# Cross-attention with LayerNorm: score matmuls cut into 32x64 tiles, two kinds of elementwise work exchanged between ScalarE and VectorE

## The chip, the cores and the metric

The kernel runs on one core of one Trainium2 chip. The metric is device time in microseconds (us) from the start to the end of one launch; the kernel before takes 534.93 us (median of 3 runs, 534.4 to 535.43). PE is TensorE (PEld its weight loads), DVE is VectorE, ACT is ScalarE, POOL is GpSimd, SP is SyncE, which issues most of the DMAs. A measurement of this kernel can tell about 0.2% from no change.

## What is computed

Four sequences of 2048 queries of width 512 attend to 77 keys each, with 16 heads of 32. The result goes through an output matrix, the input is added, and each row is normalised and scaled.

```python
qs = (x @ wq).reshape(B, 2048, 16, 32).transpose(0, 2, 1, 3)
ks_ = (ctx @ wk).reshape(B, 77, 16, 32).transpose(0, 2, 1, 3)
vs = (ctx @ wv).reshape(B, 77, 16, 32).transpose(0, 2, 1, 3)
scores = einsum('bhqd,bhkd->bhqk', qs, ks_) / sqrt(32)
scores = where(mask[:, None], -inf, scores)
attn = einsum('bhqk,bhkd->bhqd', softmax(scores), vs)
out = attn.transpose(0, 2, 1, 3).reshape(B, 2048, 512) @ wo + x
mu, var = mean(out), mean((out - mu) ** 2)
y = (out - mu) / sqrt(var + 1e-5) * gamma + beta
```

## The kernel before

The 8192 rows are 64 tiles of 128 queries. Tile t is cut out of a group of four tiles (512 queries) for the query projection, and out of a block of two tiles for everything behind the softmax. Matmuls that need more than one pass of precision are written as three products of high and low parts.

The stages of one tile, by function:

- `q_visit(g, m)` (L163): 12 matmuls, which project 512 queries of group g on 128 of the 512 columns, into one PSUM bank. `q_evac(g, m)` (L174) copies the bank to SBUF, 128x512 floats, on VectorE.
- `scores(t)` (L274): 16 matmuls, one for each head, into four PSUM banks. A head's 32 rows of the query columns sit on 32 of the 128 partitions; each matmul uses 32 rows and all 128 columns of the array, its weights are the 128 queries and 77 keys stream through. Heads j = 0 to 3 use the four row strips and write to four banks. In the trace each of these float matmuls is two weight loads and two matmuls.
- `maxima(t, lo, hi)` (L291), VectorE: for each head, one instruction adds the mask, writes the negated scores to SBUF and gives the maximum; an accumulator read follows it.
- `exps(t, lo, hi)` (L308), ScalarE: the exponential of each head with its sum.
- `recip(t)` on VectorE, `normalise(t)` (L324) on GpSimd: the probabilities over the sum, one instruction of 128x1232.
- `transp(t)` on VectorE and `regroup(b)` with 12 DMAs on SP's queue: probabilities with keys on partitions.
- `av(b)` (L374): probabilities times values for two tiles, in 96x32 tiles of the array. `av_hi` on ScalarE and `av_lo` on VectorE split the result.
- `o_proj(t)` (L436): 12 matmuls with the output matrix. `residual(t)` adds the input rows, `moments(t)` (L456) takes mean and variance on VectorE; for the second tile of a block, four short GpSimd instructions (L468 to L471) make `rn`: the factor 1/sqrt(var + eps) and the offset -mean times factor, one each for every row.
- `scale(t)` (L473): o = factor * o + offset for the 128x512 rows of a tile, in place in SBUF, on ScalarE. `affine(t)` (L479): times gamma, plus beta, two GpSimd instructions. `store(t)`: DMA to the output.
- `cast_xT` (ScalarE) and `split_xT` (L151, GpSimd, one instruction of 128x1024): high and low part of the transposed input for later projections.

The schedule is written out by hand: every engine works through its instructions in the order in which the program emits them. A loop (L583 to L687) runs for u = 0, 2, ..., 52; one turn works on tiles u and u+1 in the first stages, on u-6 and u-5 in the output projection, and, from u = 8 on, on u-8 and u-7 in `scale`, `affine` and `store`. In one turn VectorE gets: `maxima(u)` with a `q_evac` between its two halves, `residual`, `moments`, `transp(u-1)`, a second `q_evac`, `maxima(u+1)` with `recip(u)` in it, `av_lo`, `residual`, `av_lo`, `transp(u)`, `moments`, `recip(u+1)`. GpSimd gets: `normalise(u-1)` at the turn's start, `split_xT`, `affine(u-8)`, `normalise(u)`, `affine(u-7)`, the four instructions for `rn`. ScalarE gets: `cast_xT`, twelve exponentials of u, `scale(u-8)`, `scale(u-7)`, the last four of u, four of u+1, two `av_hi`, and twelve of u+1. TensorE gets: `scores(u)`, `o_proj(u-6)`, `q_visit`, `scores(u+1)`, `av`, `o_proj(u-5)`, `q_visit`. All PSUM tiles come from eight banks in turn, 14 in one turn of the loop, so that a stage waits for the reader of the tile that was given out eight before.

Three times, VectorE prepares the mask of the next sequence in a turn of its own (`mask_bias`, u = 12, 28, 44, and `mask_nan`, u = 14, 30, 46), between `transp(u-1)` and `maxima(u+1)`.

The last ten tiles and the output stages that are still open follow the string `ORDER` (L45), one word for each step, with other placements; `k` there is `scale`, `q` is `q_evac`.

Of the kernel before, what the change touches and what calls it, by code (L numbers as in the profile page):

```python
# [13 lines left out]
ALU = mybir.AluOpType  # L14
# [3 lines left out]
P = 128  # L18
D = 512
H = 16  # L20
HD = 32
NK = 77
# [4 lines left out]
GH = 4  # L27
# [3 lines left out]
BLK = 256  # L31
# [36 lines left out]
def xattn_layernorm(  # L68
# [15 lines left out]
    nc = tc.nc  # L84
    NB = mask.shape[0]
    TPB = mask.shape[2]
# [8 lines left out]
    def bank(name):  # L95
        return ps.tile([P, 512], F32, tag="mm", name=name)
# [8 lines left out]
    kct = const.tile([P, NG, NB, NK2], F32, name="kct")  # L105
# [28 lines left out]
    def keys_of(h):  # L134
        return slice(TAIL_K, NK2) if h % 2 == 0 else slice(0, NK)

    fx, gx, qd, qp, bat, pts = {}, {}, {}, {}, {}, {}
    scs, nmax, sums, bts, at, pas = {}, {}, {}, {}, {}, {}
    od, pos, mvs, rns, vd, ris, ends = {}, {}, {}, {}, {}, {}, []


    def load_xT(g, c):
        fx[g, c] = sb.tile([P, 2, GRP], F32, tag="xtf", name=f"xtf_{g}_{c}")
        nc.sync.dma_start(fx[g, c], xT[g, :, c : c + 2])

    def cast_xT(g, c):
        if g not in gx:
            gx[g] = [sb.tile([P, NC_D, GRP], F32R, tag=t, name=f"{t}_{g}") for t in ("xth", "xtl")]
        nc.scalar.copy(gx[g][0][:, c : c + 2], fx[g, c])  # L149

    def split_xT(g, c):  # L151
        h, l = (a[:, c : c + 2] for a in gx[g])
        nc.gpsimd.tensor_tensor(l, fx.pop((g, c)), h.bitcast(F32), ALU.subtract)  # L153
# [17 lines left out]
            for i in range(2):  # L171
                q_rows(pq[:, i * BLK : (i + 1) * BLK], m + i, 0, slice(BLK, GRP))

    def q_evac(g, m):  # L174
        pq = qp.pop((g, m))
        if g:
            nc.vector.tensor_copy(qd[g][:, m, :], pq)
        else:
            nc.vector.tensor_copy(qd[0][:, m : m + 2, BLK:], pq.rearrange("p (m r) -> p m r", m=2))


    def keys_part(pks, m, cs):
# [42 lines left out]
    def values_evac(b):  # L225
        pv = vd.pop(b)[:NK2].rearrange("p (q a d) -> p q a d", a=2, d=HD)
        for a in range(2):
            nc.vector.tensor_scalar(
                vsb[:, b].rearrange("p (q a d) -> p q a d", a=2, d=HD)[:, :, a], pv[:, :, a], vm[:, a, 0:1], None, ALU.mult
            )  # L230
# [42 lines left out]

    def scores(t):  # L274
        qs = qd[t // 4]
        rs = slice((t % 4) * P, (t % 4) * P + P)
        nmax[t] = sb.tile([P, H], F32, tag="nm", bufs=3, name=f"nm_{t}")
        sums[t] = sb.tile([P, H], F32, tag="sum", bufs=3, name=f"sum_{t}")
        sc = scs[t] = [bank(f"sc_{t}_{j}") for j in range(GH)]
        for g in range(NG):  # L280
            for j in range(GH):
                q = slice(HD * j, HD * (j + 1))
                nc.tensor.matmul(  # L283
                    sc[j][:, g * NK : (g + 1) * NK],
                    qs[q, g, rs],
                    kct[q, g, t // TPB, keys_of(j)],
                    start=True,
                    stop=True,
                )

    def maxima(t, lo, hi):  # L291
        pb = pbuf[t % NPB]
        mb = bat[t // TPB][0]
        nm = nmax[t]
        for h in HEADS[lo:hi]:
            g, j = divmod(h, GH)
            nc.vector.tensor_tensor_reduce(  # L297
                pb[:, h // 2, (h % 2) * NK : (h % 2 + 1) * NK],
                scs[t][j][:, g * NK : (g + 1) * NK],
                mb[:, t % TPB, keys_of(h)],  # L300
                -1.0,
                3.0e38,
                ALU.add,
                ALU.min,
                accum_out=nm[:, h : h + 1],
            )

    def exps(t, lo, hi):  # L308
        pb = pbuf[t % NPB]
        for h in HEADS[lo:hi]:  # L310
            nc.scalar.activation(  # L311
                pb[:, h // 2, (h % 2) * NK : (h % 2 + 1) * NK],
                pb[:, h // 2, (h % 2) * NK : (h % 2 + 1) * NK],
                AF.Exp,
                bias=nmax[t][:, h : h + 1],
                scale=-1.0,
                accum_out=sums[t][:, h : h + 1],
            )
# [100 lines left out]
    def load_x(t):  # L419
        if t < NT - 8:  # L420
            od[t] = sb.tile([P, D], F32, tag="o", bufs=8, name=f"o_{t}")
        elif t < NT - 4:
            if not ends:
                ends.append(sb.tile([P, NC_D, GRP], F32R, tag="xth", name="o_end").bitcast(F32))
            od[t] = ends[0][:, t % 4]
        else:
            if t % 2 == 0:
                ends.append(sb.tile([P, 2, GRP], F32, tag="xtf", name=f"o_end_{t}"))
            od[t] = ends[-1][:, t % 2]
        nc.sync.dma_start(od[t], x[t * P : (t + 1) * P, :])  # L430
# [42 lines left out]
    def scale(t):  # L473
        o = od[t]
        tt = t % 2
        rn = rns[t // 2]
        nc.scalar.activation(o, o, AF.Identity, bias=rn[:, 1, tt : tt + 1], scale=rn[:, 0, tt : tt + 1])

    def affine(t):  # L479
        o = od[t]  # L480
        nc.gpsimd.tensor_tensor(o, o, gam, ALU.mult)  # L481
        nc.gpsimd.tensor_tensor(o, o, bet, ALU.add)  # L482
# [52 lines left out]
    for c in range(NC_D):  # L535
        split(x0h[:, c], x0l[:, c], f0[c // 2 * 2][:, 0, c % 2])
        split(wqh[:, c], wql[:, c], stage_a[:, 0, c])
        for m in range(NG):
            for n, (w, r) in enumerate(((wqh, x0h), (wqh, x0l), (wql, x0h))):
# [4 lines left out]
                    start=(c == 0 and n == 0),  # L544
                    stop=(c == NC_D - 1 and n == 2),
# [30 lines left out]
    def visits(u):  # L576
        return early.get(u) or [divmod(u + 5, 4)] * (u + 5 < 4 * NGRP)

    def pieces(u):
        return casts.get(u) or [((u + 8) // 4, u % 4)] * (u + 8 < 4 * NGRP)  # L580

    evac = [(0, 0)]
    for u in range(0, 2 * CUT, 2):  # L583
        n = u // 2
        m, k = divmod(u, TPB)

        for q in pieces(u + 2):
            if u >= 4:
                load_xT(*q)
        for t in (u - 4, u - 3):  # L590
            if t >= 0:
                load_x(t)
        scores(u)
        maxima(u, 0, H // 2)
        for q in evac:
            q_evac(*q)
        maxima(u, H // 2, H)
        for q in pieces(u):
            cast_xT(*q)
        exps(u, 0, 3 * H // 4)  # L600
        for v in list(vd):
            values_evac(v)
        for q in pieces(u):
            split_xT(*q)
        if u == 0:
            mask_bias(0, slice(1, TPB))
            split_wv()
        if u >= 6:
            o_proj(u - 6)
        for v in {2: (0,), 4: (2, 3)}.get(u, ()):  # L610
            values(v)
        for q in visits(u):
            q_visit(*q)
        if u >= 6:
            residual(u - 6)
            moments(u - 6)
        if u == 4:
            transp(2)
        if u:
            transp(u - 1)  # L620
            regroup(n - 1)
        if u >= 8:
            scale(u - 8)
            scale(u - 7)
        exps(u, 3 * H // 4, H)
        if u >= 8:
            affine(u - 8)
        for q in visits(u):
            q_evac(*q)
        if u == 0:  # L630
            load_wo()
            nc.gpsimd.memset(ident, 0.0)
            nc.gpsimd.affine_select(ident, ident, [[-1, P]], ALU.not_equal, 1.0, base=0, channel_multiplier=1)
        if u == 2:
            split_wo(0)
            split_wo(1)
        if k == TPB - 6 and m + 1 < NB:
            load_mask(m + 1)
        if k == TPB - 4 and m + 1 < NB:
            mask_bias(m + 1)  # L640
        if k == TPB - 2 and m + 1 < NB:
            mask_nan(m + 1)

        scores(u + 1)
        maxima(u + 1, 0, 3 * H // 4)
        recip(u)
        maxima(u + 1, 3 * H // 4, H)
        exps(u + 1, 0, H // 4)
        normalise(u)
        if u >= 8:  # L650
            affine(u - 7)
        for v in list(vd):
            values_evac(v)
        if u >= 4:
            av(n - 2)
            av_hi(n - 2, 0)
            av_hi(n - 2, 1)
        exps(u + 1, H // 4, H)
        if u >= 5:
            o_proj(u - 5)  # L660
        if u >= 4:
            av_lo(n - 2, 0)
        if u >= 5:
            residual(u - 5)
        if u >= 4:
            av_lo(n - 2, 1)
        if u != 2:
            transp(u)
        for v in {2: (1,)}.get(u, ()):
            values(v)  # L670
        evac = visits(u + 1)
        for q in evac:
            q_visit(*q)
        if u == 2:
            load_xT(*pieces(4)[0])
        if u >= 5:
            moments(u - 5)
        if u == 0:
            mask_nan(0)
        if u == 2:  # L680
            split_wo(2)
            split_wo(3)
        recip(u + 1)
        normalise(u + 1)
        if u >= 8:
            store(u - 8)
            store(u - 7)  # L687
# [87 lines left out]
```

## Time and profile before

| | |
|---|---|
| median of 3 runs | 534.93 us |
| span of the profiled execution | 533.1 us |
| PE busy | 522.3 us (98%) |
| DVE busy | 486.2 us (91%) |
| ACT busy | 459.6 us (86%) |
| POOL busy | 400.7 us (75%) |
| score matmuls (L283) | 2048 records, 72.5 us |
| copies of projected queries (L177) | 60, 669 ns each |
| `scale` (L477) | 48, 807 ns each |

The profiled execution's span is 1.8 us under the median of the timed runs. Busy time is the union of the instructions of an engine, which overlap their neighbours a little; the pitch from one start to the next is what an instruction costs in a row of its kind. Rows of a timeline give start, duration, engine, line, operation and tile, and in brackets the idle time before the instruction with what ended it. The chain of waits follows the work that ended last backwards.

### The profile page before, as it was taken

The page shows a single profiled execution, that of the slowest core. Times are in us where ns is not written, and L with a number is a line of the kernel's source. Part 1 is how long each engine was busy: PE and PEld are TensorE (multiplying, and loading weights), DVE is VectorE, ACT ScalarE, POOL GpSimd, SP SyncE. Part 2 cuts the span into 40 slices and gives each one's busy share as a digit, 9 for nine tenths or more (in the row PEclk, how much of TensorE's full clock was granted, in tenths as well). Part 3 has the DMA queues.
Part 4 walks back from the last instruction along what each step waited for, and adds up shares of the span by engine and source line. Part 5 has one row for each costly group of instructions (what it writes and reads, how often), then busy time and mean ns, then how long its engine had stood idle before and what let it go on. Part 6 is the DMA issues. An engine that isn't in the chain of part 4 may idle for free.

```text
span 533.1 us, 16107 instructions
## 1 busy us (share of the span) xinstructions
PE 522.3 (98%) x4810; PEld 399.1 (75%) x4810; DVE 486.2 (91%) x2592; ACT 459.6 (86%) x2215; POOL 400.7 (75%) x363
## 2 busy tenths in 40 slices
PE   8999999999999999999999999999999999999994
PEld 6977777777777777777777777777777777776672
DVE  5689989999998889889998998889999989999897
ACT  6687799999899999998899999998899999998600
POOL 0626547998798988887899888888799888665751
PEclk9999999999999999999999999999999999999997
DMA  8934667788677887787677787867687775849744
GB/s 300 402 120 111 202 173 195 222 232 226 176 187 213 227 215 208 208 226 201 179 213 214 208 221 217 232 165 211 191 216 216 219 191 159 219 129 281 226 138 157
DMA packets 58695, 109.96 MB, mean 206 GB/s; under 512 B 9392, under 2 KB 11056, under 8 KB 58608
## 3 DMA queue, kind: packets, MB, share of 16 engines
q1 hardware_dynamic: 55424, 102.64, 68.6%
q0 software_dynamic: 2304, 5.24, 3.5%
q10 hardware_dynamic: 880, 1.05, 0.7%
q8 instruction: 38, 0.62, 0.5%
q14 instruction: 49, 0.40, 0.2%
HBM read 41.79 MB, written 16.78 MB: 110 GB/s over the span
## 4 chain that ended last, share of the span: by engine, by line
PE 88%; DMA 5%; DVE 4%; issue 1%; SPq 1%; ACT 0%; DVEq 0%
PE pq L160 32%; PE po L445 30%; PE sc L283 12%; PE pa L381 9%; DMA PT<-B 2%; PE pv L221 2%; DMA out<-o 2%; PE pk L186 1%; DVE B L351 1%; DVE pbuf L297 1%; DMA stage_a<-wq 1%; PE pq L540 1%; DVE o_end L504 1%; DVE o_end L501 1%; SPq L363 0%
## 5 line engine op out<-in xcount | busy, mean ns | idle before, releaser
L311 ACT ACTIVATE pbuf<-pbuf,nm 128x77 f32<-128x77 f32 x1024 | 352.9, 352 | 31.4 <-DVE nm L297 26.5
L311 ACT ACTIVATION_READ_ACCUMULATOR pbuf<-pbuf,nm 128x1 f32 x1024 | 197.3, 193 | 0.0
L327 POOL TENSOR_TENSOR pbuf<-pbuf,ri 128x1232 f32<-128x1232 f32 x63 | 142.9, 2268 | 61.1 <-DVE ri L322 47.4
L297 DVE CUSTOM_DVE_ANT_0 pbuf<-sc,mb 128x77 f32<-128x77 f32 x1024 | 169.0, 231 | 4.9 <-PE sc L283 3.3
L445 PE MATMUL po<-woh,AH 128*128 128x512 f32 x256 | 108.6, 424 | 0.0
L445 PE MATMUL po<-wol,AH 128*128 128x512 f32 x256 | 100.4, 392 | 0.0
L445 PE MATMUL po<-woh,AL 128*128 128x512 f32 x256 | 100.1, 391 | 0.0
L160 PE MATMUL pq<-xth,wqh 128*128 128x512 f32 (+1 forms) x256 | 98.4, 385 | 0.0
L160 PE MATMUL pq<-xtl,wqh 128*128 128x512 f32 (+1 forms) x256 | 97.9, 382 | 0.0
L160 PE MATMUL pq<-xth,wql 128*128 128x512 f32 (+1 forms) x256 | 97.8, 382 | 0.0
L351 DVE STREAM_TRANSPOSE B<-pbuf 128x1280 f32<-128x1280 f32 x64 | 95.5, 1493 | 1.9 <-POOL pbuf L327 1.8
L297 DVE DVE_READ_ACCUMULATOR2_ANT nm<- 128x1 f32 x1024 | 84.0, 82 | 0.0
L283 PEld LDWEIGHTS sc<-kct,q 32*128 32x128 f32 x2048 | 63.0, 186 | 22.6 <-issue 12.0
L283 PE MATMUL sc<-kct,q 32*128 32x77 f32 x2048 | 72.5, 277 | 0.0
L153 POOL TENSOR_TENSOR xtl<-xtf,xth 128x1024 fp32r<-128x1024 f32 x28 | 67.1, 2397 | 1.9 <-ACT xth L149 1.9
L482 POOL TENSOR_TENSOR o<-o,bet 128x512 f32<-128x512 f32 x48 | 63.1, 1314 | 3.8
L445 PEld LDWEIGHTS po<-woh,AH 128*128 128x128 f32 x256 | 48.0, 187 | 23.1 <-DVE nm L297 6.6
L481 POOL TENSOR_TENSOR o<-o,gam 128x512 f32<-128x512 f32 x48 | 61.6, 1284 | 0.2
L381 PE MATMUL pa<-PT,vsb 96*32 96x256 f32 x992 | 60.0, 382 | 1.6 <-DMA out<-o 0.9
L445 PEld LDWEIGHTS po<-woh,AL 128*128 128x128 f32 x256 | 48.1, 188 | 10.7
L160 PEld LDWEIGHTS pq<-xth,wqh 128*128 128x128 f32 x256 | 48.1, 188 | 10.2 <-DVE nm L297 0.4
L445 PEld LDWEIGHTS po<-wol,AH 128*128 128x128 f32 x256 | 48.1, 188 | 9.6 <-issue 1.4
(106 smaller groups left out, 664.4 us busy)
## 6 DMA issues: line engine op xcount, KB each, us to landing
PT<-B SPq DMA_DIRECT2D x346, 128.0 KB, 2.4
xtf<-xT SPq DMA_DIRECT2D x28, 512.0 KB, 4.8
o<-x SPq DMA_DIRECT2D x56, 256.0 KB, 4.9
out<-o SPq DMA_DIRECT2D x56, 256.0 KB, 2.9
PT<-B POOLq DMA_DIRECT2D x21, 128.0 KB, 5.2
o_end<-x SPq DMA_DIRECT2D x8, 256.0 KB, 5.4
out<-o_end SPq DMA_DIRECT2D x8, 256.0 KB, 2.4
xtf<-xT SPq DMA_DIRECT2D x4, 256.0 KB, 5.0
```

What stands on the lines that cost most here:

```text
L153: nc.gpsimd.tensor_tensor(l, fx.pop((g, c)), h.bitcast(F32), ALU.subtract)
L160: nc.tensor.matmul(pq, w[:, c, m * P : (m + 1) * P], r[:, c, rs], start=(n == 0), stop=(n == 11))
L221: nc.tensor.matmul(pv[:NK2, :], ctx_s[c][i][:, b, :], v[c], start=(n == 0), stop=(n == 11))
L283: nc.tensor.matmul(sc[j][:, g * NK : (g + 1) * NK], qs[q, g, rs], kct[q, g, t // TPB, keys_of(j)], start=True, stop=True,)
L297: nc.vector.tensor_tensor_reduce(pb[:, h // 2, (h % 2) * NK : (h % 2 + 1) * NK], scs[t][j][:, g * NK : (g + 1) * NK], mb[:, t % TPB, keys_ ...
L311: nc.scalar.activation(pb[:, h // 2, (h % 2) * NK : (h % 2 + 1) * NK], pb[:, h // 2, (h % 2) * NK : (h % 2 + 1) * NK], AF.Exp, bias=nmax[t ...
L327: nc.gpsimd.tensor_tensor(pv, pv, rv.to_broadcast((P, NP, 2, NK)), ALU.mult)
L351: nc.vector.transpose(bt.rearrange("p c q r -> p q c r"), pbuf[t % NPB].rearrange("p q (c r) -> p q c r", c=5),)
L381: nc.tensor.matmul(pas[b, g // 2][HD * j : HD * (j + 1), (g % 2) * BLK : (g % 2 + 1) * BLK], vsb[:, 2 * b // TPB, HD * h : HD * (h + 1)], ...
L445: nc.tensor.matmul(pos[t], a[:, c, rs], w[:, c, :], start=(first and c == 0 and n == 0), stop=(c == NC_D - 1 and n == 2),)
L481: nc.gpsimd.tensor_tensor(o, o, gam, ALU.mult)
L482: nc.gpsimd.tensor_tensor(o, o, bet, ALU.add)
```

## The change

Three edits. The score matmuls of a tile are issued in two halves of 64 queries: 32 in place of 16 for each tile, each with 32 rows and 64 columns of the array, so that the second half writes to partitions 64 to 127 of the same banks. In the loop the copies of projected queries move from VectorE to ScalarE, at the same places of the program (`q_evac` in `ORDER` stays on VectorE). And in the loop `scale` is replaced by `rescale`, the same arithmetic as one VectorE instruction with two operands that hold a value for each row; both tiles' instructions stand right behind `maxima(u)`, ahead of `residual(u-6)`. `scale` in `ORDER` (tiles 46 and 47) stays on ScalarE.

```diff
-    def q_evac(g, m):
+    def q_evac(g, m, copy=nc.vector.tensor_copy):
         pq = qp.pop((g, m))
         if g:
-            nc.vector.tensor_copy(qd[g][:, m, :], pq)
+            copy(qd[g][:, m, :], pq)
         else:
-            nc.vector.tensor_copy(qd[0][:, m : m + 2, BLK:], pq.rearrange("p (m r) -> p m r", m=2))
+            copy(qd[0][:, m : m + 2, BLK:], pq.rearrange("p (m r) -> p m r", m=2))
...
-        rs = slice((t % 4) * P, (t % 4) * P + P)
...
         for g in range(NG):
-            for j in range(GH):
-                q = slice(HD * j, HD * (j + 1))
-                nc.tensor.matmul(
-                    sc[j][:, g * NK : (g + 1) * NK],
-                    qs[q, g, rs],
-                    kct[q, g, t // TPB, keys_of(j)],
+            for half in range(0, P, P // 2):
+                for j in range(GH):
+                    q = slice(HD * j, HD * (j + 1))
+                    r0 = (t % 4) * P + half
+                    nc.tensor.matmul(
+                        sc[j][half : half + P // 2, g * NK : (g + 1) * NK],
+                        qs[q, g, r0 : r0 + P // 2],
+                        kct[q, g, t // TPB, keys_of(j)],
...
+    def rescale(t):
+        o = od[t]
+        tt = t % 2
+        rn = rns[t // 2]
+        nc.vector.tensor_scalar(o, o, rn[:, 0, tt : tt + 1], rn[:, 1, tt : tt + 1], ALU.mult, ALU.add)
...
         maxima(u, 0, H // 2)
         for q in evac:
-            q_evac(*q)
+            q_evac(*q, nc.scalar.copy)
         maxima(u, H // 2, H)
+        if u >= 8:
+            rescale(u - 8)
+            rescale(u - 7)
...
-        if u >= 8:
-            scale(u - 8)
-            scale(u - 7)
         exps(u, 3 * H // 4, H)
         if u >= 8:
             affine(u - 8)
         for q in visits(u):
-            q_evac(*q)
+            q_evac(*q, nc.scalar.copy)
```

More of the change, by code (lines that the diff above doesn't have):

```diff
@@ L280, in scores @@
         for g in range(NG):
-            for j in range(GH):
-                q = slice(HD * j, HD * (j + 1))
-                nc.tensor.matmul(
-                    sc[j][:, g * NK : (g + 1) * NK],
-                    qs[q, g, rs],
-                    kct[q, g, t // TPB, keys_of(j)],
-                    start=True,
-                    stop=True,
-                )
+            for half in range(0, P, P // 2):
[6 more added lines that the diff above has]
+                        kct[q, g, t // TPB, keys_of(j)],
+                        start=True,
+                        stop=True,
+                    )
     def maxima(t, lo, hi):
```

## The prediction

> **What bounds the kernel now.** I read the page first: busy times and the chain of waits, by engine and by line.
>
> ```profile
> span 533.1 us, 16107 instructions
> PE 522.3 (98%) x4810; PEld 399.1 (75%) x4810; DVE 486.2 (91%) x2592; ACT 459.6 (86%) x2215; POOL 400.7 (75%) x363
> ...
> PE 88%; DMA 5%; DVE 4%; issue 1%; SPq 1%; ACT 0%; DVEq 0%
> ```
>
> TensorE is busy all the time and is the chain, but VectorE's 91% is an average: it has less than a tenth to give. Second, the chain in order of time around one turn of the loop (start, us, what), with a row of the tail.
>
> ```profile
> 202.71 1.06 PE sc L283 x32
> ...
> 209.41 1.06 PE sc L283 x32
> 210.47 1.86 PE pa L381 x32
> ...
> 218.00 1.06 PE sc L283 x32
> ...
> 515.97 1.93 PE pa L396 x64
> ```
>
> A turn is 218.00 - 202.71 = 15.29 us of TensorE without a hole, 2 x 1.06 of it scores. Third, VectorE's timeline in the same turn.
>
> ```profile
> 203.44 0.22 DVE L322 RECIPROCAL ri<-sum 128x16 f32<-128x16 f32 x1
> 203.78 0.24 DVE L297 CUSTOM_DVE_ANT_0 pbuf<-sc,mb 128x77 f32<-128x77 f32 x1
> ...
> 205.06 0.69 DVE L177 COPY q<-pq 128x512 f32<-128x512 f32 x1
> 205.66 0.23 DVE L297 CUSTOM_DVE_ANT_0 pbuf<-sc,mb 128x77 f32<-128x77 f32 x1
> ...
> 206.92 0.69 DVE L454 TENSOR_TENSOR o<-po,o 128x512 f32<-128x512 f32 x1
> ...
> 209.87 0.65 DVE L177 COPY q<-pq 128x512 f32<-128x512 f32 x1
> 210.48 0.24 DVE L297 CUSTOM_DVE_ANT_0 pbuf<-sc,mb 128x77 f32<-128x77 f32 x1
> ...
> 213.13 0.69 DVE L416 TENSOR_TENSOR AL<-pa,AH 128x512 fp32r<-128x512 f32 x1
> 215.32 0.69 DVE L454 TENSOR_TENSOR o<-po,o 128x512 f32<-128x512 f32 x1 [1.50 <-PE po L445]
> ...
> 218.74 0.22 DVE L322 RECIPROCAL ri<-sum 128x16 f32<-128x16 f32 x1
> ```
>
> From reciprocal to reciprocal it is 15.30 us too. VectorE's own slack is the wait for `po`, 1.59 us counted from the pitch (213.13 + 0.60 to 215.32), and 0.17 at 203.61, where the pitch of a reciprocal would have ended and the score matmuls had not. So VectorE needs 13.54 us a turn. The question is what the change does to that number.
>
> **Scores in 32x64 tiles.** No row shows this shape. The nearest are the weight loads and the `pa` stages.
>
> ```profile
> L283 PEld LDWEIGHTS sc<-kct,q 32*128 32x128 f32 x2048 | 63.0, 186 | 22.6 <-issue 12.0 <-PE pq L160 4.2 <-DVE nm L297 2.6
> ...
> L381 PEld LDWEIGHTS pa<-PT,vsb 96*32 96x32 f32 x992 | 29.4, 109 | 20.8 <-DVE o L501 1.2 <-DMA PT<-B 1.1 <-DVE nm L297 0.4
> ```
>
> A score stage is 32 records on four row strips, so 8 steps of 1.06/8 = 0.132 us. A `pa` stage runs on four column strips: 8 steps of 1.86/8 = 0.232 with 256 columns streaming, 16 steps of 1.93/16 = 0.121 with 128 (the row of 515.97). That is 0.00087 us a column, and 0.077 for 77 columns. A score step takes 0.055 more than this, and the weight load is what differs: 186 ns for 128 columns against 109 for 32. With 64 columns the load is some 135 ns by these two rows, 51 less, so that a step comes near 0.08. The change doubles the records (64 a stage), but on eight tiles of the array, so again 8 steps if all eight run together: 0.62 us a stage. If the two column halves ran one after the other it would be 1.23, and if each step kept its price 2.12. I take 0.70, since the `pa` rows show column strips side by side, with 0.08 for the longer stagger: -0.36 a stage, -0.72 a turn. TensorE then needs 14.57 us a turn.
>
> **Copies to ScalarE, `scale` away from it.** ScalarE's price of a copy from PSUM is that of the cast of the same shape.
>
> ```profile
> L412 ACT CAST AH<-pa 128x512 fp32r<-128x512 f32 x64 | 34.1, 574 | 15.0 <-PE pa L396 12.5 <-PE pa L381 2.0 <-DVE st L490 0.4
> L477 ACT ACTIVATE o<-o,rn 128x512 f32<-128x512 f32 x48 | 36.4, 807 | 0.0
> L311 ACT ACTIVATE pbuf<-pbuf,nm 128x77 f32<-128x77 f32 x1024 | 352.9, 352 | 31.4 <-DVE nm L297 26.5
> ```
>
> Two copies of 0.53 (34.1/64) replace two scalings of 0.76 (36.4/48): -0.45 us a turn on ScalarE. The copied banks are read a whole projection before anyone needs them, so nothing is queued on them for long. VectorE gives up its two copies: 205.06 to 205.66 and 209.87 to 210.48, -1.21 us. Without its slack VectorE would then need 13.54 - 1.21 = 12.33.
>
> **`rescale` on VectorE.** It is two TENSOR_SCALAR of 128x512, SBUF to SBUF. What such an instruction does beside a busy GpSimd stands in two places of the trace, the mask preparations, and beside an idle one in a third.
>
> ```profile
> 27.68 0.31 DVE L265 TENSOR_SCALAR mb<-m 128x285 bf16<-128x285 uint8 x1
> ...
> 117.77 1.27 POOL L481 TENSOR_TENSOR o<-o,gam 128x512 f32<-128x512 f32 x1
> 118.56 1.14 DVE L264 TENSOR_SCALAR mb<-m 128x1232 bf16<-128x1232 uint8 x1
> 119.11 1.72 POOL L482 TENSOR_TENSOR o<-o,bet 128x512 f32<-128x512 f32 x1
> 119.62 1.39 DVE L265 TENSOR_SCALAR mb<-m 128x304 bf16<-128x304 uint8 x1
> ...
> 134.62 1.42 DVE L269 TENSOR_REDUCE nz<-m 128x16 f32<-128x1232 uint8 x1
> 135.37 1.28 POOL L482 TENSOR_TENSOR o<-o,bet 128x512 f32<-128x512 f32 x1
> 136.07 0.61 DVE L270 TENSOR_SCALAR nz<-nz 128x16 f32<-128x16 f32 x1
> 136.72 0.18 DVE L271 TENSOR_SCALAR nz<-nz 128x16 f32<-128x16 f32 x1
> ```
>
> L265 takes 0.31 us alone and 1.39 beside L482, and ends 0.18 after it (121.01 against 120.83). L270 ends 0.03 after L482 (136.68 against 136.65), and its twin L271 takes 0.18. L264 ends 0.66 after L481; L482, issued meanwhile, takes 1.72 in place of 1.28 and ends 1.13 after L264. So a TENSOR_SCALAR in SBUF and a GpSimd instruction exclude each other: the later one waits for the whole earlier one, and then they alternate; L265, right behind L264, had to let L482 pass first. The Trainium skill, "SBUF — State Buffer", section "Who interferes with whom", says it as a rule: copy and tensor_scalar with both ends in SBUF can use a second port pair that belongs to GpSimd too, and whoever has it keeps it for the whole instruction. The rows agree; that it holds for operands with a value for each row, no row here shows. By the rule the page also has the removed copies, which read PSUM, free of it.
>
> Now GpSimd in the same turn.
>
> ```profile
> 203.60 0.20 POOL L468 TENSOR_TENSOR rn<-mv,nz 128x2 f32<-128x2 f32 x1 [1.29 <-DVE mv L464]
> ...
> 205.08 2.26 POOL L327 TENSOR_TENSOR pbuf<-pbuf,ri 128x1232 f32<-128x1232 f32 x1
> 207.30 2.41 POOL L153 TENSOR_TENSOR xtl<-xtf,xth 128x1024 fp32r<-128x1024 f32 x1
> 209.65 1.28 POOL L481 TENSOR_TENSOR o<-o,gam 128x512 f32<-128x512 f32 x1
> ```
>
> Its phase hangs on VectorE's: the `rn` instructions start 0.16 behind the reciprocal's start, once the last mean and variance are there. The 16 maxima take 1.28 + 1.26 (203.78 to 205.06, 205.66 to 206.92); with the reciprocal's 0.17, VectorE comes to the first `rescale` 2.71 after 203.44, at 206.15. By then `rn` is ready (205.08), and L327 runs until 207.34: a wait of 1.19. An instruction then costs 0.27 (512 x 0.66/1232, from L264) + 0.03: 207.64. L153 has been issued meanwhile and goes first: 2.41 less 0.15 (L482's 1.28 against 1.13 behind L264), until 209.90; the second `rescale` ends at 210.20. VectorE has lost 210.20 - 206.15 = 4.05 us, 0.6 of it work. Its turn is 12.33 + 4.05 = 16.38 us: over TensorE's 14.57, so that VectorE becomes the bound and TensorE's gain falls into a gap.
>
> Behind the two instructions are queued `residual`, `moments`, `transp` and `maxima(u+1)`; ScalarE waits for the last, and TensorE's second `o_proj` for the bank that `residual` frees. From the first maximum of u+1 ScalarE needs 0.35 until it starts, 16 x 0.345 (352.9/1024) for its exponentials and 1.06 for the two casts, 6.93 in all, before the turn's last reciprocal; VectorE's own way there is (213.73 - 210.48) + (218.74 - 215.32) = 6.67. So a turn is 16.38 to 16.64, and I take 16.5: +1.2 on 15.30. If `rescale` cost as much as the copies it replaces (0.69), it would be +1.9.
>
> **What else moves.** The mask turns were hidden in the 1.59 us of slack, which is gone. At the new place GpSimd has finished L481 and L482 before VectorE arrives (their 2.6 us behind 210.20 end at 212.8; VectorE comes there 206.92 to 209.87 = 2.95 behind, 213.15), so the instructions cost what they cost alone: 0.66 + 0.31 for the bias, 1.42 + 2 x 0.18 and small gaps for the other, together 2.8, three times: +8.4 (6 if a part is still covered, 14 at the prices of the rows above). In the turns u = 0 to 6 there is no `rescale`, and TensorE stays the bound: 8 stages x -0.36 = -2.9. In `ORDER` VectorE has nothing to spare and its work is the same; of the ten faster stages I count -1 (0 to -3.6).
>
> **The sum.** `rescale` stands in the turns u = 8 to 52, which are 23: 23 x 1.2 = +27.6 (24.8 at 16.38, 43.7 at +1.9). +8.4 - 2.9 - 1.0 makes +32.1. The profiled span of 533.1 goes to 565.2; the median of the timed runs lies 534.93 - 533.1 = 1.8 above the span, so 567.0.
>
> **The rivals.**
>
> No exclusion: `rescale` with a value for each row uses one port, or waits for nobody. For it: no row has that form; against it: all six mask preparations behind a busy GpSimd look like the two above. VectorE's turn would be 12.33 + 2 x 0.3 to 0.6 = 12.9 to 13.5, TensorE's 14.57 stays the bound, and some 57 stages that lie on the chain save 0.36: -20, so 515. This is the case on the other side; it decides as long as VectorE's turn stays under 14.57.
>
> One wait only: the second `rescale` gets in before L153. VectorE is free at 207.94, its turn is 14.1, TensorE is the bound again, and only the mask turns run over it (15.1 and 15.9: 3 x (0.5 + 1.3) = 5.4): 520. Against it: L265 behind L264 lost to L482 where GpSimd's next instruction was queued, as L153 is.
>
> TensorE worse: the tiles don't overlap and a stage takes 2.12. Then TensorE's turn is 15.29 + 2 x 1.06 = 17.4, over VectorE's, and 64 x 1.06 = 68: 603. Against it: the `pa` rows. At 1.06 to 1.23 a stage TensorE's turn is at most 15.6 and VectorE remains the bound; the time is then 570 to 573, within the forecast's range.
>
> **How the numbers follow.** The forecast has 0.82, no exclusion 0.09, one wait 0.06, TensorE worse 0.03. The forecast's own range is its terms at their ends, not all at once: 24.8 + 6 - 3.5 - 3.6 = +24 gives 558.6, and 43.7 + 8.4 - 3.9 = +48 gives 583; turns that recover some slack at the loop's ends could take away 8 more. So 550 to 585, which leaves out the faster rivals (0.15), the worst (0.03) and little else. Within 0.2%, about what a measurement of this kernel can tell from no change, lies none of the cases: 0.01. Faster 0.15, slower 0.84.
>
> **What would show it.** In the profile after: a turn of about 16.5 us; the first `rescale` some 1.5 us long and ending just behind L327, the second some 2.5 us and ending just behind L153; VectorE near 100% in the loop and TensorE with a hole of some 2 us in each turn, ahead of the second `o_proj`; score stages of about 0.7. If the `rescale` rows are 0.3 to 0.6 us and TensorE has no hole, the exclusion is wrong; if VectorE has holes instead, it is ScalarE or GpSimd that ends last and my turn is too simple.

## The result and the profile after

The changed kernel takes 571.69 us (median of 4 runs, 571.01 to 574.47) against 535.18 for the kernel before beside it: a ratio of 1.0693, 95% interval 1.0675 to 1.0711. It is 36.5 us slower; 567 had been forecast, with 550 to 585 as the range. The page of the changed kernel, in the lines that answer to those of before:

```profile
span 569.2 us, 20410 instructions
PE 524.0 (92%) x6858; PEld 398.3 (70%) x6858; DVE 540.1 (95%) x2582; ACT 454.0 (80%) x2225; POOL 407.4 (72%) x363
...
DVE 51%; ACT 30%; PE 10%; DMA 3%; POOL 2%; issue 2%; SPq 1%; DVEq 0%; ACTq 0%; POOLq 0%
...
L484 DVE TENSOR_SCALAR o<-o,rn 128x512 f32<-128x512 f32 x46 | 92.5, 2050 | 0.0
...
L284 PE MATMUL sc<-kct,q 32*64 32x77 f32 x4096 | 64.0, 238 | 1.4 <-DVE nm L298 1.4
```

The chain has left TensorE (88% before, 10% now) for VectorE and ScalarE. The 46 `rescale` instructions are recorded with 2.05 us each. VectorE's timeline of one turn (start, us, engine, line, operation) shows where:

```profile
200.54 0.25 DVE L323 RECIPROCAL ri<-sum 128x16 f32<-128x16 f32 x1
...
203.19 4.03 DVE L484 TENSOR_SCALAR o<-o,rn 128x512 f32<-128x512 f32 x2
207.14 0.68 DVE L455 TENSOR_TENSOR o<-po,o 128x512 f32<-128x512 f32 x1
...
208.68 1.48 DVE L352 STREAM_TRANSPOSE B<-pbuf 128x1280 f32<-128x1280 f32 x1
...
216.98 0.25 DVE L323 RECIPROCAL ri<-sum 128x16 f32<-128x16 f32 x1
```

GpSimd and TensorE in the same stretch:

```profile
202.16 2.26 POOL L328 TENSOR_TENSOR pbuf<-pbuf,ri 128x1232 f32<-128x1232 f32 x1
204.37 2.56 POOL L153 TENSOR_TENSOR xtl<-xtf,xth 128x1024 fp32r<-128x1024 f32 x1
206.90 1.45 POOL L488 TENSOR_TENSOR o<-o,gam 128x512 f32<-128x512 f32 x1
```

```profile
203.62 0.95 PE L284 MATMUL sc<-kct,q 32*64 32x77 f32 x64
...
207.87 0.50 PE L446 MATMUL po<-woh,AH 128*128 128x512 f32 x1 [1.14 <-DVE o L455]
```

The pair of `rescale` starts at 203.19, in the middle of L328; it ends at 207.22, just behind L153, which ends at 206.93. In narrower windows the two stand one by one:

```profile
203.19 1.51 DVE L484 TENSOR_SCALAR o<-o,rn 128x512 f32<-128x512 f32 x1
...
204.62 2.60 DVE L484 TENSOR_SCALAR o<-o,rn 128x512 f32<-128x512 f32 x1
```

The first ends at 204.70, 0.28 us behind L328 (204.42), the second 0.29 behind L153. L153, which was issued before the first had ended, is recorded with 2.56 us in place of 2.41. In each of the 23 turns the two end 0.28 to 0.29 us behind these two GpSimd instructions. TensorE then has its hole ahead of the second `o_proj`, which waits for the bank that `residual` (L455) frees.

The difference is found stretch by stretch, by the reciprocals that begin the turn u = 8 and the tail:

```profile
82.94 0.25 DVE L323 RECIPROCAL ri<-sum 128x16 f32<-128x16 f32 x1
...
468.86 0.25 DVE L323 RECIPROCAL ri<-sum 128x16 f32<-128x16 f32 x1
```

In the kernel before:

```profile
83.00 0.25 DVE L322 RECIPROCAL ri<-sum 128x16 f32<-128x16 f32 x1
...
433.37 0.22 DVE L322 RECIPROCAL ri<-sum 128x16 f32<-128x16 f32 x1
```

Up to u = 8 nothing changes (-0.06 us), the 23 turns with `rescale` take 385.92 in place of 350.37 (+35.55), and the rest 569.2 - 468.86 = 100.3 in place of 99.7 (+0.6).

### The profile page after: what moved, and what is told of

Read it like the earlier page. It is cut to its first block, busy times and chain, and to the rows that moved or that the text cites. A ratio compares the mean times of both kernels' runs of the same rounds, so it can differ in the third digit from the quotient of the medians.

```text
span 569.2 us, 20410 instructions
## 1 busy us (share of the span) xinstructions
PE 524.0 (92%) x6858; PEld 398.3 (70%) x6858; DVE 540.1 (95%) x2582; ACT 454.0 (80%) x2225; POOL 407.4 (72%) x363
## 4 chain that ended last, share of the span: by engine, by line
DVE 51%; ACT 30%; PE 10%; DMA 3%; POOL 2%; issue 2%; SPq 1%; DVEq 0%; ACTq 0%; POOLq 0%
ACT pbuf L312 26%; DVE o L484 16%; DVE pbuf L298 13%; DVE B L352 8%; ACT AH L413 4%; PE po L446 3%; DVE st L460 3%; DVE o L455 3%; POOL pbuf L328 2%; DVE ri L323 1%; PE pk L186 1%; DMA PT<-B 1%; DVE nm L298 1%; PE pq L547 1%; PE pa L382 1%
## 5 line engine op out<-in xcount | busy, mean ns | idle before, releaser
L328 POOL TENSOR_TENSOR pbuf<-pbuf,ri 128x1232 f32<-128x1232 f32 x63 | 142.8, 2267 | 103.0 <-DVE ri L323 90.2
L298 DVE CUSTOM_DVE_ANT_0 pbuf<-sc,mb 128x77 f32<-128x77 f32 x1024 | 165.8, 229 | 3.1 <-PE sc L284 3.1
L446 PE MATMUL po<-woh,AH 128*128 128x512 f32 x256 | 110.4, 431 | 22.3 <-DVE o L455 22.3
L446 PE MATMUL po<-wol,AH 128*128 128x512 f32 x256 | 101.9, 398 | 0.0
L446 PE MATMUL po<-woh,AL 128*128 128x512 f32 x256 | 101.9, 398 | 0.0
L484 DVE TENSOR_SCALAR o<-o,rn 128x512 f32<-128x512 f32 x46 | 92.5, 2050 | 0.0
L153 POOL TENSOR_TENSOR xtl<-xtf,xth 128x1024 fp32r<-128x1024 f32 x28 | 71.1, 2542 | 1.2 <-ACT xth L149 1.2
L284 PEld LDWEIGHTS sc<-kct,q 32*64 32x64 f32 x4096 | 52.9, 130 | 25.0 <-issue 17.8
L488 POOL TENSOR_TENSOR o<-o,gam 128x512 f32<-128x512 f32 x48 | 65.9, 1372 | 0.0
L284 PE MATMUL sc<-kct,q 32*64 32x77 f32 x4096 | 64.0, 238 | 1.4 <-DVE nm L298 1.4
```

What stands on the lines that cost most here:

```text
L284: nc.tensor.matmul(sc[j][half : half + P // 2, g * NK : (g + 1) * NK], qs[q, g, r0 : r0 + P // 2], kct[q, g, t // TPB, keys_of(j)], start= ...
L298: nc.vector.tensor_tensor_reduce(pb[:, h // 2, (h % 2) * NK : (h % 2 + 1) * NK], scs[t][j][:, g * NK : (g + 1) * NK], mb[:, t % TPB, keys_ ...
L328: nc.gpsimd.tensor_tensor(pv, pv, rv.to_broadcast((P, NP, 2, NK)), ALU.mult)
L446: nc.tensor.matmul(pos[t], a[:, c, rs], w[:, c, :], start=(first and c == 0 and n == 0), stop=(c == NC_D - 1 and n == 2),)
L484: nc.vector.tensor_scalar(o, o, rn[:, 0, tt : tt + 1], rn[:, 1, tt : tt + 1], ALU.mult, ALU.add)
```

## The experiments

Eight kernels, each beside the kernel before. The first four take the change apart and move the suspected collision; the last four test the price of `rescale` alone and what the score tiles are worth.

**Tiles alone.** The kernel before with the new `scores` and nothing else.

```diff
-            for j in range(GH):
+            for half in range(0, P, P // 2):
+                for j in range(GH):
```

> The kernel before with the 32x64 score tiles alone; copies of projected queries stay on VectorE, the LayerNorm scaling on ScalarE. Theory (VectorE's waits behind GpSimd in rescale made the change slower, the tiles are a small gain): a score stage shrinks from 1.06 to about 0.88 us as in the profile after, TensorE's turn from 15.29 to 14.93, VectorE's need of 13.54 stays under it except in the mask turns; 535 - 8 to - 10 + about 3 there = 527 to 531. Rival (the doubled matmuls themselves slow the kernel, or drain TensorE): at or above 535.

Measured: 534.01 us against 535.13, ratio 0.9974 (0.9965 to 0.9984). The tiles do no harm, so they are not the loss; but they give 1.1 us where 4 to 8 were expected. Stretch by stretch, by the same reciprocals in the profiled executions, it is +0.39 up to u = 8, -1.72 in the 23 turns and -0.7 behind them. The experiment after next shows where the gain in a turn goes.

**Scaling back on ScalarE.** The changed kernel with `rescale` undone.

```diff
-        if u >= 8:
-            rescale(u - 8)
-            rescale(u - 7)
...
+        if u >= 8:
+            scale(u - 8)
+            scale(u - 7)
         exps(u, 3 * H // 4, H)
```

> The changed kernel with rescale alone undone: scaling back on ScalarE, tiles and copies as changed. Theory: VectorE's turn falls from 16.44 to 12.4 us, TensorE's is 14.93; ScalarE now has the copies as well as the scaling, 14.4 + 1.06 = 15.46 a turn, and bounds: about 535 to 540. Rival (the copies on ScalarE, by holding back exponentials, or the tiles make the loss): 560 or more.

Measured: 538.89, ratio 1.0075 (1.0060 to 1.0090). With 33 us gone, the loss is in `rescale` or its place; the copies on ScalarE and the tiles together cost 3.8 us. In the profiled execution 1.3 us more than before lie ahead of u = 8 (84.29 in place of 83.00). ScalarE carries copies and scaling here and is busy throughout, 268.00 of the 268 us between 150 and 418 in the table by windows.

**`rescale` a little later.** The same two instructions on VectorE, behind `transp(u-1)` in place of ahead of `residual`.

```diff
         maxima(u, H // 2, H)
-        if u >= 8:
-            rescale(u - 8)
-            rescale(u - 7)
...
             regroup(n - 1)
+        if u >= 8:
+            rescale(u - 8)
+            rescale(u - 7)
```

> The changed kernel with both rescale instructions moved behind transp(u-1), nothing else. There GpSimd is at the end of split_xT, and its next instruction (affine) waits for rescale itself, so that it cannot go between the two. Theory: the first waits some 0.6 us, both run in about 0.3 each, VectorE's turn is 12.33 + 1.2 = 13.5, TensorE's 14.93 is the bound again: 527, plus or minus 3. Rival 1 (the instruction is slow by itself, some 2 us with operands for each row): VectorE's turn stays at 16.4, time near 571. Rival 2 (TensorE loses by the tiles or the copies): above 535 with rescale rows of 0.3.

Measured: 538.22, ratio 1.0064 (1.0048 to 1.0079), 11 us over the expected middle, but 33 under the changed kernel, by a move of two instructions. VectorE and then GpSimd in the timeline of one turn:

```profile
319.69 0.96 DVE L484 TENSOR_SCALAR o<-o,rn 128x512 f32<-128x512 f32 x2
```

```profile
317.44 2.39 POOL L153 TENSOR_TENSOR xtl<-xtf,xth 128x1024 fp32r<-128x1024 f32 x1
320.28 1.52 POOL L488 TENSOR_TENSOR o<-o,gam 128x512 f32<-128x512 f32 x1 [0.45 <-DVE o L484]
```

In this turn both `rescale` instructions take 0.96 us together: the split ends 0.14 us after the first starts, and GpSimd's next instruction waits for `rescale`, not the other way round. It is issued once the first `rescale` is done, while the second runs, and is recorded with 1.52 us in place of the 1.28 of before. So the instruction is not slow by itself. In 11 of the 23 turns the pair takes 0.96 to 0.97 us; in the other 12 the split has more left to do when the first `rescale` comes, which then ends 0.28 to 0.29 us behind it, and the pair takes 1.3 to 1.6. VectorE's busy time is 485.9 us, where the changed kernel has 540.1. What stays above the expectation is in the main TensorE, as in the second rival, whose chain in order of time reads:

```profile
205.84 0.88 PE sc L284 x52
206.72 2.93 PE po L446 x12
209.65 2.72 PE pq L160 x12
212.37 0.97 PE sc L284 x52
213.34 0.24 issue
213.59 1.93 PE pa L382 x32
215.52 2.96 PE po L446 x12
...
221.20 0.88 PE sc L284 x53
```

The first score stage of the turn takes 0.88 us in place of 1.06. The second takes 0.97, then TensorE stands for 0.24 on `issue`, which is a wait for nothing that the profile shows, and `pa` takes 1.93 in place of 1.86: 3.14 where the kernel before has 2.92. This turn is 221.20 - 205.84 = 15.36 us, against 15.29 before. From the score stage of u = 8 (83.67) to that of tile 54 (434.88) the mean turn is 15.27; in the kernel before (80.02 to 432.57) it is 15.33, so that hardly any of the gain is left. By VectorE's reciprocals the 23 turns take 351.21 us, where 14.93 a turn would be 343.4: 7.8 of the 11 us. The time up to u = 8 is 84.47 in place of 83.00, and the rest 101.2 in place of 99.7; a cause for the first is below, under the copies, the second I did not follow.

**The split later.** The changed kernel with `rescale` where it was, but `split_xT` behind `affine(u-8)` in GpSimd's order.

```diff
-        for q in pieces(u):
-            split_xT(*q)
...
             affine(u - 8)
+        for q in pieces(u):
+            split_xT(*q)
```

> The changed kernel with split_xT moved behind affine(u-8) in GpSimd's order, so that nothing is ready to run on GpSimd between the two rescale instructions; rescale stays where the change put it. Theory (two waits, the second is L153's): the first wait of 1.2 us behind normalise stays, the second is gone, VectorE's turn is 16.44 - 2.3 = 14.1, TensorE's 14.93 bounds except in the mask turns: about 531, 527 to 535. Rival (the second instruction's 2.6 us are not GpSimd's split but its own cost or any GpSimd work that follows): near 571, with the second rescale still at 2 us or more.

Measured: 538.67, ratio 1.0088 (1.0059 to 1.0117). GpSimd and VectorE in one turn:

```profile
209.16 2.26 POOL L328 TENSOR_TENSOR pbuf<-pbuf,ri 128x1232 f32<-128x1232 f32 x1
211.78 1.53 POOL L488 TENSOR_TENSOR o<-o,gam 128x512 f32<-128x512 f32 x1 [0.36 <-DVE o L484]
...
214.63 2.40 POOL L153 TENSOR_TENSOR xtl<-xtf,xth 128x1024 fp32r<-128x1024 f32 x1
```

```profile
210.19 1.97 DVE L484 TENSOR_SCALAR o<-o,rn 128x512 f32<-128x512 f32 x2
```

The first wait is still there, until L328 ends at 211.42; the second is gone, 1.97 us for the pair against 4.03. VectorE's instructions are the same and in the same order as in the changed kernel; a change in GpSimd's order alone takes off 33 us. The time lies above the expected 527 to 535, as in the experiment before: the 23 turns take 351.94 us, and the time up to u = 8 is 85.27 in place of 83.00.

**`rescale` alone.** The kernel before with the change's `rescale` and its place, copies on VectorE, tiles as before.

```diff
         maxima(u, H // 2, H)
+        if u >= 8:
+            rescale(u - 8)
+            rescale(u - 7)
...
-        if u >= 8:
-            scale(u - 8)
-            scale(u - 7)
```

> The kernel before with rescale alone, where the change put it: score tiles as before, copies of projected queries on VectorE. Theory: the second rescale ends where GpSimd's normalise and split let it, whatever VectorE does before; with the copy in front the first arrives 0.6 us later and waits 0.6 less, and VectorE's turn is 13.54 + 3.45 = 17.0 us; 535 + 23 x 1.7 + 8 in the mask turns = 582, 576 to 588, slower than the whole change. Rival (a part of the loss comes from the copies on ScalarE or the tiles): at or under 571.

Measured: 583.44, ratio 1.0887 (1.0848 to 1.0925). In the chain of waits:

```profile
308.93 0.25 DVE ri L322
...
312.25 3.34 DVE o L483 x2
...
325.95 0.25 DVE ri L322
```

A turn is 17.02 us, as expected (17.0). With the copy in front, `rescale` starts 3.32 behind the reciprocal and takes 3.34 by the chain (3.24 and 3.43 by the timeline); in the changed kernel these are 2.65 and 4.03 by the timeline. Both end 6.66 to 6.68 behind the reciprocal: the end is GpSimd's. So moving the copies, with the tiles, gives 11.8 us back where VectorE is the bound.

**32x32 tiles.** The kernel before with quarters in place of halves: 128 pairs of weight load and matmul a stage.

```diff
+            for half in range(0, P, P // 4):
```

> The kernel before with the score matmuls as 32x32 tiles: 64 matmuls a stage, 128 pairs of weight load and matmul, nothing else. In the profile after, the first 32 pairs of a 32x64 stage start within 0.3 to 0.4 us, eight tiles abreast, and the other 32 one pair every 0.0167 us. Theory (instructions reach TensorE at that rate, and only what is queued ahead goes faster): 0.35 + 96 x 0.0167 + 0.15 = 2.1 us a stage against 1.06, TensorE's turn 17.4, some 57 stages on the chain: 535 + 59 = 594, 580 to 605. Rival (the array sets the pace; sixteen tiles take 8 steps of about 0.11): 0.9 to 1.05 us a stage, 528 to 535.

Measured: 596.4, ratio 1.1108 (1.1050 to 1.1166). The profiled execution is longer than the median (span 606.7), so I read only the lengths of single stages from it, in the chain of waits:

```profile
306.15 1.67 PE sc L284 x85
307.82 0.05 issue
307.87 1.50 PE pa L382 x24
309.37 0.79 issue
310.16 0.64 PE pa L382 x8
```

The time is as expected, the working only in part: a stage is 1.50 to 1.68 us and not 2.1, which over 57 stages makes 25 to 35 of the 61 us, and a part of the rest is in holes around `pa`. That the number came out is partly luck. By the start times of single records in the trace, the 128 matmuls of a stage start within 1.34 us, the first 32 of them within 0.19; the 64 of a 32x64 stage within 0.73, the first 32 within 0.30; the 32 of a 32x128 stage within 0.86. So smaller tiles do run side by side, but behind the first 32 pairs the rate is one pair in 0.012 (1.15/96) to 0.013 us (0.43/32), for tiles of either size. The constant rate of 0.0167 that the expectation used does not hold; in the changed kernel's profile, too, the other 32 pairs of most stages are 0.013 us apart.

**Tiles in even stages.** The kernel before with 32x64 tiles for even t alone, so that the stage ahead of `av` keeps 32 pairs.

```diff
+        step = P // 2 if t % 2 == 0 else P
         for g in range(NG):
-            for j in range(GH):
+            for half in range(0, P, step):
+                for j in range(GH):
```

> The kernel before with 32x64 tiles in the first score stage of a turn alone (even tiles); the second, which av follows, keeps 32x128. Theory: the tiles shorten the first stage to 0.88 us; in the second stage the gain is lost because the four waits in front of av, read ahead while 32 pairs run, are reached only after 64 pairs have been fed, and stand open for some 0.24 us. So the second stage and av return to 1.06 + 1.86, the turn is 15.29 - 0.18 = 15.11: 535 - 4 = 531, 529 to 532, faster than the tiles in both (534). Rival (the tiles gain nothing in either, the 1 us of that run came from elsewhere): 534 to 535.

Measured: 532.12, ratio 0.9935 (0.9914 to 0.9956), faster than with tiles in both stages, at the upper end of the expected 529 to 532. The chain:

```profile
308.02 0.88 PE sc L285 x54
308.90 2.96 PE po L447 x12
311.86 2.72 PE pq L160 x12
314.58 1.06 PE sc L285 x32
315.64 1.86 PE pa L383 x32
317.51 2.95 PE po L447 x12
...
323.17 0.88 PE sc L285 x54
```

The second stage and `pa` are back at 1.06 and 1.86, without a hole, and the turn is 15.15 us.

**A combined version.** `rescale` behind `transp(u-1)`, tiles in even stages, copies on ScalarE from u = 8 on.

```diff
         for q in evac:
-            q_evac(*q, nc.scalar.copy)
+            q_evac(*q, nc.scalar.copy if u >= 8 else nc.vector.tensor_copy)
```

> A version for speed: 32x64 tiles in even stages alone, rescale behind transp(u-1), copies on ScalarE from u = 8 on and on VectorE before (the early turns keep ScalarE full). Theory: TensorE's turn 15.11 is the bound, VectorE needs 13.5, ScalarE about 14: 531, 529 to 533. Rival (moving the copies costs something in every turn, by the banks that are read later): 535 or more.

Measured: 531.95, ratio 0.9944 (0.9922 to 0.9966). It beats both kernels of the case, and is not told apart from the even tiles alone: its turn is TensorE's too (0.88 at 307.46 to 0.88 at 322.61 in its chain, 15.15 us), so the room on VectorE that the new place of `rescale` and the copies leave buys nothing.

## Why the prediction was right

**The exclusion.** The step that carried the sum was the two waits behind GpSimd, worked out as 4.05 us a turn, with a first `rescale` of some 1.5 us that ends just behind L327 and a second of some 2.5 that ends just behind L153. The rows show 1.51 and 2.60, and these ends. Measured, VectorE comes to `rescale` at 203.19 and to the next instruction at 207.14, 3.95. The two experiments that keep the instruction but take away GpSimd's part, by place and by GpSimd's order, remove 33 of the 36.5 us, and `rescale` alone is enough for a loss of 48. That it holds for operands with a value for each row, which no row before showed, is now seen: the pair of 4.03 us becomes 0.96 where GpSimd has all but done and its next instruction waits. By this the rule of the Trainium skill, "SBUF — State Buffer", section "Who interferes with whom", that whoever has the shared port pair keeps it for the whole instruction, agrees with the traces for this form too: 4.03 us for the pair behind two GpSimd instructions, 1.97 behind one, 0.96 behind the last 0.14 us of one.

**The turn.** Forecast 16.5, measured 216.98 - 200.54 = 16.44 in the turn shown. ScalarE's exponentials ahead of the reciprocal are on the chain with VectorE (30% for ScalarE, 51% for VectorE), as worked out: the two paths through the second half of a turn lay 0.26 us apart. The forecast had TensorE's hole at about 2 us; the row of the hole shows 1.14, since TensorE's work was not cut to 14.57: with the small hole ahead of `pa` (0.23) it stayed at 16.44 - 1.14 = 15.30.

**The mask turns.** Forecast +2.8 for each pair. The last reciprocal of three turns, in VectorE's timeline of the changed kernel:

```profile
115.69 0.25 DVE L323 RECIPROCAL ri<-sum 128x16 f32<-128x16 f32 x1
...
133.05 0.25 DVE L323 RECIPROCAL ri<-sum 128x16 f32<-128x16 f32 x1
...
151.22 0.25 DVE L323 RECIPROCAL ri<-sum 128x16 f32<-128x16 f32 x1
```

Turns of 17.36 and 18.17, together 2.65 over two of 16.44. Together with the turn: +36.0 forecast for the 23 turns, +35.55 measured.

**The score tiles.** This term was mis-sized. It put a stage at 0.70 us in place of 1.06, -0.72 a turn, -2.9 in the early turns and -1 in the tail. A first stage takes 0.88; in the second, with `pa` behind it, the gain is more than lost, and TensorE's turn stayed at 15.3. The early turns gave -0.06 and the tail +0.6, together 4.4 us more than forecast. With 0.5 less in the loop, and 0.7 more in the distance between span and median (1.8 before, 2.5 after), this is the way from 567 to 571.7.

The working had priced the array's steps by stages in which the pairs start 0.027 us apart or more (0.86/32 in a score stage); what happens when they come closer, no row of before showed. In the early turns the forecast also had TensorE as the only bound. With the tiles alone these turns take 0.39 us more than before, and not 2.9 less; the chain of waits between 48 and 86 us, TensorE's throughout in the kernel before, is there to 48.5% ScalarE's exponentials, and to 45.5% in the changed kernel. How the early turns come to their time is not settled by this.

In the trace of the kernel with `rescale` a little later, TensorE's queue has four semaphore waits between the last weight load of the scores (212.96) and the first load of `pa` (213.56), 0.11 to 0.26 us apart, and no other load in this stretch. That these, read late behind 64 pairs, are the hole of 0.24 us is argued, not shown: the even tiles show only that the hole goes with the doubled stage ahead of `pa`. That a change of tile shape by itself makes such a hole is unlikely, since the first stage goes over to `o_proj` without one.

**The copies.** The group of the 54 copies is recorded with 30.7 us on ScalarE, 0.57 each (0.53 forecast). The working said of the copied banks that nothing is queued on them for long. In the turn u = 4 this failed; ScalarE and then TensorE in the changed kernel:

```profile
62.05 0.57 ACT L177 COPY q<-pq 128x512 f32<-128x512 f32 x1
```

```profile
62.67 1.07 PE L382 MATMUL pa<-PT,vsb 96*32 96x256 f32 x16 [2.26 <-ACT q L177]
```

The copy stands behind exponentials, with ScalarE busy for the whole 4 us between 60 and 64, and the second half of `av` waits for it for 2.26 us. The three other kernels that copy on ScalarE from the start have the same wait, of 2.24 to 2.81 us; in the kernel before, with tiles alone and in the combined version TensorE is busy throughout these 4 us. In the kernel with `rescale` a little later this wait is on the chain, and the projection behind it takes 4.43 us in place of 2.72, with a granted clock of 0.74 between 64 and 70 us. In the changed kernel the time up to u = 8 is no longer for it (-0.06), but where VectorE was not the bound the copies were a loss: with the scaling back on ScalarE the kernel took 538.9, with tiles alone 534.0. Copied on ScalarE from u = 8 on only, as in the combined version, they cost nothing that can be told.

## What to carry to other kernels

Before moving an in-place scaling from ScalarE to VectorE, look at what GpSimd runs at that moment: VectorE may wait for the rest of the GpSimd instruction, and a second one right behind waits for the next whole one. Put such instructions where GpSimd's next work depends on them, or is not ready; the same instructions cost 4.0 us a turn in one place and 1.0 to 1.6 a few instructions later. A copy that frees a PSUM bank can hold up TensorE when it moves to an engine that is full just then. And a cut of matmuls into more and smaller tiles has to be priced with the work that follows it on TensorE's queue, not by the array alone.

## What the runs showed of the hardware

Two things were not expected. In a stage of 64 or 128 pairs of load and matmul the first 32 start within 0.30 and 0.19 us, and the rest go on at 0.012 to 0.013 us a pair, for either size of tile; 32x64 tiles brought 0.18 us of the 0.36 expected in a first stage, and 32x32 tiles cost some 0.5 us a stage. And `rescale` on 128x512 floats, with at most the end of GpSimd's split beside it, is recorded with 0.50 to 0.54 us, and its successor starts 0.42 to 0.45 after it, more than the 0.30 that the forecast had from the mask preparations; behind a wait only 0.3 of it is left after GpSimd's end.
